# Which operand stands still: the gate and up products of a mixture of experts, f32, on one core

## The chip, the core and the metric

The kernel runs on one core of one Trainium2 chip. Its time is the device time of one execution in microseconds; of several runs the median is given. The engines are TensorE (matmul, with its weight loads listed apart as PEld), VectorE (DVE), ScalarE (ACT), GpSimd (POOL) and SyncE (SP, which here only issues transfers).

## What is computed

One block of a perceiver: attention from 2 x 512 tokens of 512 features to 2 x 8192 context rows, a windowed self-attention, and a mixture of experts. The change lies in the last part, which the reference writes as

```python
scores = jax.nn.sigmoid(h @ gate_w.T)
topk_score, topk_ids = jax.lax.top_k(scores.T, cap)        # cap = 128
xin = h[topk_ids]                                          # 16 experts x 128 tokens x 512
up = jnp.einsum('ecd,efd->ecf', xin, up_w) + up_b[:, None, :]
g = jnp.einsum('ecd,efd->ecf', xin, gw) + gb[:, None, :]
eo = jax.nn.silu(g) * up                                   # 2048 features per token
eo = jnp.einsum('ecf,edf->ecd', eo, down_w) + down_b[:, None, :]
flat = (eo * topk_score[..., None]).reshape(-1, Dm)
out = jnp.zeros_like(h).at[topk_ids.reshape(-1)].add(flat)
```

plus a shared expert that every token passes. All of it is f32.

## The kernel before

The program is one stream of stages. The attention to the context fills the span up to some 2640 us, the windowed attention goes up to some 2860 us, the shared expert up to 3033 us, and the sixteen experts take the rest. The source order, as the scheduler of the framework has laid it out per engine, sets the order of the work; each engine then runs its own list in order and waits for the others by semaphores. The two orders differ in places: transposes can come some matmuls earlier than the source has them.

An expert has 128 tokens, which is one tile. `gather(e)` fetches their rows from HBM by an indirect transfer on POOL's queue. `tokens(xin)` turns them with four transposes on TensorE and one copy on ScalarE (`transposed`, lines 94 to 99), so that features lie on partitions: `xinT` is 128 x 4 x 128.

The 2048 features of an expert's gate and up are worked in four quarters of 512 (`fq`). For each, `expert_in` loads one 1 MB tile of gate weights and one of up weights (`load_tile`, on SP's queue, nine buffers in two pools). Each of the two products is five matmuls into one PSUM bank `pf` of 128 tokens x 512 features. The first adds the bias: the stationary operand `pick` selects the expert's row, the moving operand `bias3` holds the biases, split in three bf16 parts on 96 partitions so that their sum is the f32 value. The other four, one for each 128 of the 512 input features, have the tokens `xinT` as stationary operand and 512 columns of weights as moving operand. ScalarE makes `sg`, the silu of gate (line 924), and VectorE multiplies it by up into `eo` (line 926).

`eo` has tokens on partitions, and the down product needs features there. So the loop at the end turns each quarter with four transposes and a copy on ScalarE into `eoT`, one quarter behind the products. After the fourth quarter `expert_out` makes the down product: a bias matmul from `pick` and `bias3`, sixteen matmuls of 512 columns with `eoT` stationary and four more weight tiles moving, a scaling by the token's score, and an indirect transfer that adds to the output.

The biases are made ready much earlier, beside the windowed attention, at places that `at(k, ...)` gives: `bias_in` fills `raw` with zeros and loads the rows three times on POOL's queue, and `bias_part` splits off one bf16 part on VectorE (a cast, a copy, and but for the last a subtraction). Gate's and up's rows are 2048 wide, down's 512. In the same stretch TensorE runs the windowed attention's own products, among them `pl` (line 624) and `plv` (line 634), the latent projections of keys and values, which wait for ScalarE and VectorE.

Of the kernel before, what the change touches and what calls it, by code (L numbers as in the profile page):

```python
# [10 lines left out]
F32 = mybir.dt.float32  # L11
I32 = mybir.dt.int32
U32 = mybir.dt.uint32
BF16 = mybir.dt.bfloat16
AF = mybir.ActivationFunctionType
ALU = mybir.AluOpType
# [3 lines left out]
P = 128  # L20
B, S, D = 2, 512, 512
# [4 lines left out]
DC = D // P  # L26
# [6 lines left out]
E, F, SH, CAP = 16, 2048, 1024, 128  # L33
FQ = F // 512
# [9 lines left out]
def perceiver_kernel(  # L44
# [8 lines left out]
    nc = tc.nc  # L53
# [40 lines left out]
    def transposed(dst, src, ps):  # L94

        tp = ps.tile([P, 4, P], F32, tag="ps", name="tp")
        for c in range(4):
            nc.tensor.transpose(tp[:, c, :], src[:, ts(c, P)], ident)  # L98
        nc.scalar.copy(dst, tp)
# [17 lines left out]
    with ExitStack() as es:  # L117
        cp = es.enter_context(tc.tile_pool(name="a_const", bufs=1))
        tmp = es.enter_context(tc.tile_pool(name="a_tmp", bufs=2))
# [8 lines left out]
        ps = first_ps.enter_context(tc.tile_pool(name="a_ps1", bufs=1, space=PSUM))  # L128
# [317 lines left out]
        for slot in range(NS + LAG):  # L446
            if slot == LAG:
                first_ps.close()
                steady_ps = ExitStack()
                ps = ps_q = steady_ps.enter_context(tc.tile_pool(name="a_ps", bufs=8, space=PSUM))  # L450
            if slot == NS + LAG - NKC:
                steady_ps.close()
                ps = es.enter_context(tc.tile_pool(name="a_ps3", bufs=7, space=PSUM))
# [51 lines left out]
    def load_tile(src):  # L505
        pool, tag = ((ctxp, "ctx"), (wpool, "w"))[loads[0] % 9 >= 4]
        loads[0] += 1
        t = pool.tile([P, 4, 512], F32, tag=tag, name="wt")
        nc.sync.dma_start(out=t, in_=src)
        return t  # L510

    ccp = ctx.enter_context(tc.tile_pool(name="c_const", bufs=1))
    ctmp = ctx.enter_context(tc.tile_pool(name="c_tmp", bufs=2))
    ps = ctx.enter_context(tc.tile_pool(name="c_ps", bufs=8, space=PSUM))
    dram = ctx.enter_context(tc.tile_pool(name="c_dram", bufs=1, space=bass.MemoryType.DRAM))
    h_dram = dram.tile([T, D], F32, name="h_dram")

    KB3 = 96  # L520
    FB = 2 * F + D
    pick = ccp.tile([KB3, E, P], BF16, name="pick")
    bias3 = ccp.tile([KB3, FB], BF16, name="bias3")
    gate_sb = ccp.tile([P, DC, E], F32, name="gate_sb")
    nc.gpsimd.dma_start(out=gate_sb, in_=gate.rearrange("(c p) e -> p c e", p=P))
    idx = ccp.tile([P, E], U32, name="idx")
# [12 lines left out]
    with ExitStack() as es:  # L539
        cp = es.enter_context(tc.tile_pool(name="b_const", bufs=1))  # L540
        tmp = es.enter_context(tc.tile_pool(name="b_tmp", bufs=2))
        gp = es.enter_context(tc.tile_pool(name="b_g", bufs=3))
        bp = es.enter_context(tc.tile_pool(name="b_bias", bufs=1))
# [12 lines left out]
        for h in range(4):  # L556
            r = slice(h * DK, (h + 1) * DK)
# [8 lines left out]
            out=band, in_=band, pattern=[[1, NK]], base=0, channel_multiplier=-1,  # L566
# [3 lines left out]
            out=band, in_=band, pattern=[[-1, NK]], base=W7 - 1, channel_multiplier=1,  # L570
# [160 lines left out]
        def at(k, f, *args):  # L731
            beside.setdefault(k, []).append(lambda: f(*args))
# [7 lines left out]
                pick[r], ident[r, ds(32 * i, E)].unsqueeze(2).to_broadcast([32, E, P])  # L740
            )

        def bias_in(src, n):
            raw = bp.tile([KB3, F], F32, name="raw")
            nc.gpsimd.memset(raw, 0.0)
            for i in range(3):
                nc.gpsimd.dma_start(out=raw[ds(32 * i, E), 0:n], in_=src)
            raws.append(raw)

        def bias_part(i, lo, n):  # L750
            raw = raws[-1]
            part = bp.tile([KB3, F], BF16, name="part")
            nc.vector.tensor_copy(part[:, 0:n], raw[:, 0:n])
            r = ds(32 * i, 32)
            nc.vector.tensor_copy(bias3[r, ds(lo, n)], part[r, 0:n])
            if i < 2:
                nc.vector.tensor_tensor(raw[:, 0:n], raw[:, 0:n], part[:, 0:n], ALU.subtract)

        def forward_in(n, key):

# [8 lines left out]
        lns, raws = {"b0": ln_b0}, []  # L769
# [2 lines left out]
            at(k, lambda n: attention_in(n, lns["b1"]), NT // B + i)  # L772
        for i in range(3):
            at(3 + 2 * i, picks, i)
        k = 9
        for src, lo, n in ((gb, 0, F), (up_b, F, F), (down_b, 2 * F, D)):
            at(k, bias_in, src, n)
            for i in range(3):
                k += 2
                at(k, bias_part, i, lo, n)  # L780
        at(29, norm, 0, "f0")
        for i, k in enumerate((31, 33, 35, 37)):
            at(k, forward_in, i, "f0")
# [5 lines left out]
        for k in range(len(items) + 3):  # L789
            i, n = divmod(k, NBQ)  # L790
# [54 lines left out]
    def gather(e):  # L845

        xin = ep.tile([P, D], F32, name="xin")
        nc.gpsimd.indirect_dma_start(  # L848
            out=xin, out_offset=None, in_=h_dram,
            in_offset=bass.IndirectOffsetOnAxis(ap=idx[:, e : e + 1], axis=0),  # L850
        )
        return xin

    def tokens(xin):
        xinT = ep.tile([P, DC, CAP], F32, name="xinT")
        transposed(xinT, xin, ps)
        return xinT
# [3 lines left out]
    tmp = ctmp  # L861
    ep = ctx.enter_context(tc.tile_pool(name="e_tmp", bufs=2))
    shd = [load_tile(sh_d[i]) for i in range(2)]
    norm(1, "f1")
    for b in range(B):
        sT = sTp.tile([P, SH // P, S], F32, tag="sT", name="sT")
        for f in range(SH // P):
            pair = []
            for wts in (shg, shu):
                pf = ps.tile([P, S], F32, tag="ps", name="pf")  # L870
                for c in range(DC):
                    nc.tensor.matmul(  # L872
                        pf, lhsT=wts[f // 4][:, c, ts(f % 4, P)], rhs=hT[b][:, c, :],
                        start=(c == 0), stop=(c == DC - 1),
                    )
                pair.append(pf)
            sg = st.tile([P, S], F32, name="sg")
# [7 lines left out]
            elif b == 1 and f == SH // P - 1:  # L885

                turned_lists()
                xin = gather(0)
# [3 lines left out]
        for j in range(4):  # L892
            po = ps.tile([P, D], F32, tag="ps", name="pso")
            for f in range(SH // P):
                nc.tensor.matmul(  # L895
                    po, lhsT=sT[:, f, ts(j, P)], rhs=shd[f // 4][:, f % 4, :],
                    start=(f == 0), stop=(f == SH // P - 1),
                )
            n = b * 4 + j
# [5 lines left out]
            elif j == 2:  # L905
                xinT = tokens(xin)

    def expert_in(e, fq, xinT):

        pair = []  # L910
        for src, lo in ((gw, 0), (up, F)):
            wt = ahead.pop(0) if ahead else load_tile(src[e, fq])
            pf = ps.tile([P, 512], F32, tag="ps", name="pf")
            nc.tensor.matmul(
                pf, lhsT=pick[:, e, :], rhs=bias3[:, ds(lo + fq * 512, 512)],
                start=True, stop=False,
            )
            for c in range(DC):
                nc.tensor.matmul(  # L919
                    pf, lhsT=xinT[:, c, :], rhs=wt[:, c, :], start=False, stop=(c == DC - 1)  # L920
                )
            pair.append(pf)
        sg = tmp.tile([P, 512], F32, name="sg")
        nc.scalar.activation(sg, pair[0], AF.Silu)  # L924
        eo = tmp.tile([P, 512], F32, name="eo")
        nc.vector.tensor_tensor(eo, pair[1], sg, ALU.mult)  # L926
        return eo

    def expert_out(e, eoT):
        py = ps.tile([P, D], F32, tag="ps", name="py")  # L930
        nc.tensor.matmul(
            py, lhsT=pick[:, e, :], rhs=bias3[:, ds(2 * F, D)], start=True, stop=False
        )
        for fq in range(FQ):
            wt = load_tile(down[e, fq])
            for c in range(4):
                nc.tensor.matmul(  # L937
                    py, lhsT=eoT[:, fq * 4 + c, :], rhs=wt[:, c, :],
                    start=False, stop=(fq == FQ - 1 and c == 3),
                )  # L940
        y = tmp.tile([P, D], F32, name="y")
        nc.vector.tensor_scalar(y, py, scol[:, e : e + 1], None, ALU.mult)  # L942
        nc.gpsimd.indirect_dma_start(  # L943
            out=out, out_offset=bass.IndirectOffsetOnAxis(ap=idx[:, e : e + 1], axis=0),
            in_=y, in_offset=None, compute_op=ALU.add,
        )

    eoT, done = None, None  # L950
    for k in range(E * FQ + 1):
        e, fq = divmod(k, FQ)
        if e < E:
            if fq == 0 and e > 0:
                xinT = nxt
            if fq == 0 and e + 1 < E:
                xin = gather(e + 1)
            eo = expert_in(e, fq, xinT)
        if k > 0:
            pe, pfq = divmod(k - 1, FQ)  # L960
            if pfq == 0:
                eoT = ep.tile([P, F // P, CAP], F32, name="eoT")
            transposed(eoT[:, ts(pfq, 4), :], done, ps)
            if pfq == FQ - 1:
                expert_out(pe, eoT)
        done = eo
        if fq == FQ - 1 and e + 1 < E:
            nxt = tokens(xin)

# [48 lines left out]
```

## Time and profile before

| | |
|---|---|
| Median of 3 runs | 3776.33 us (3776.25 to 3777.41) |
| Profiled execution | 3775.76 us, span 3774.0 us |
| Mean granted clock of TensorE | 0.996 |
| TensorE, matmuls busy | 3720.3 us, 99% of the span |
| VectorE / ScalarE / GpSimd busy | 2250.9 / 1614.9 / 2076.8 us |
| First gate matmul of the experts to the last down matmul | 3033.4 to 3764.6 us |
| Moved by DMA while the experts run | some 287 GB/s at a DMA share of 0.85 |

In a row of groups, the first number after the bar is the time in which at least one instruction of the group ran, the second the mean length of one in ns, and what follows the second bar is the idle time of the engine just before them and what ended it. A shape such as `128*128 128x512` gives the stationary operand (rows * columns) and the moving one. In the timeline the first number is the start, the second the length of a merged row, and `x5` the number of instructions in it. Of a matmul the end is modelled, so lengths overlap; the starts are measured. Busy time of TensorE is therefore no measure of how fast it works.

### The profile page before, as it was taken

How to read it: one execution, taken by the hardware profiler on the slowest of the kernel's cores; microseconds unless marked ns; L12 is line 12 of the kernel's file. 1: busy time of each engine (PE TensorE's matmuls, PEld its weight loads, DVE VectorE, ACT ScalarE, POOL GpSimd, SP SyncE). 2: the span in 40 equal slices, each digit the busy share in tenths (PEclk: the TensorE clock that was granted, in tenths of full speed). 3: DMA queues.
4: the chain of work that ended last, by engine and by line, in shares of the span. 5: the costliest groups of instructions: out<-in, count | busy, mean ns of one | idle time of the engine just before them, and what ended most of it. 6: DMA issues, size and time to landing. Idle time of an engine off the chain costs nothing.

```text
span 3774.0 us, 102663 instructions
## 1 busy us (share of the span) xinstructions
PE 3720.3 (99%) x44684; PEld 1854.2 (49%) x44684; DVE 2250.9 (60%) x5349; ACT 1614.9 (43%) x3020; POOL 2076.8 (55%) x562
## 2 busy tenths in 40 slices
PE   8999999999999999999999999999999999999998
PEld 4555555555555555555555555444454444444444
DVE  6877777777777777777777777687753500000000
ACT  2135555555555555555555555577462011111110
POOL 0059989998998998999899899500100000000000
PEclk9999999999999999999999999999999999999999
DMA  5322222122223432122222222122210178888885
GB/s 193 115 66 69 72 72 72 60 69 72 72 70 115 127 119 92 61 69 72 72 72 62 67 72 72 58 86 71 75 46 23 64 262 282 289 289 286 287 284 172
DMA packets 143748, 438.29 MB, mean 116 GB/s; under 512 B 9408, under 2 KB 11728, under 8 KB 117856
## 3 DMA queue, kind: packets, MB, share of 16 engines
q1 hardware_dynamic: 137856, 419.33, 33.5%
q0 software_dynamic: 5200, 12.30, 1.3%
q8 instruction: 350, 5.73, 0.6%
q14 instruction: 102, 0.84, 0.1%
q10 hardware_dynamic: 240, 0.08, 0.0%
HBM read 423.21 MB, written 8.47 MB: 114 GB/s over the span
## 4 chain that ended last, share of the span: by engine, by line
PE 94%; DVE 2%; ACT 2%; issue 1%; POOL 1%; DMA 0%; POOLq 0%; SPq 0%; ACTq 0%; DVEq 0%
PE sx L307 12%; PE pk L248 12%; PE sc L365 12%; PE pv L265 12%; PE av L389 11%; PE pf L919 11%; PE py L937 5%; PE pf L872 3%; PE sc L371 3%; PE sx L288 2%; PE avl L389 2%; PE pqkv L597 2%; PE pso L895 1%; PE po L106 1%; PE tp L98 1%
## 5 line engine op out<-in xcount | busy, mean ns | idle before, releaser
L403 POOL TENSOR_TENSOR acc<-acc,pt 128x2048 f32<-128x2048 f32 x437 | 1991.0, 4556 | 189.3 <-ACT pt L378 187.0
L378 ACT ACTIVATE pt<-sc,mbias 128x512 f32<-128x512 f32 x2016 | 1220.1, 688 | 943.4 <-PE sc L371 943.2
L312 DVE CUSTOM_DVE_ANT_0 junk<-sx,mk 128x512 bf16<-128x512 f32 x1776 | 1227.3, 691 | 538.6 <-PE sx L307 343.5
L365 PE MATMUL sc<-qT,kt 32*128 32x512 f32 x4096 | 548.3, 596 | 5.9 <-DVE vt L272 5.9
L265 PEld LDWEIGHTS pv<-wv_sb,ctx_t 128*32 128x32 f32 x16384 | 457.8, 110 | 178.9 <-DVE mst L312 106.2
L307 PE MATMUL sx<-kt,qT 32*128 32x512 f32 x3552 | 508.2, 640 | 0.9 <-DVE vt L272 0.9
L248 PE MATMUL pk<-ctx_t,wk_sb 128*32 128x256 f32 (+1 forms) x9216 | 499.7, 357 | 5.4 <-DMA ctx_t<-in_ctxT 3.1
L265 PE MATMUL pv<-wv_sb,ctx_t 128*32 128x128 f32 x16384 | 500.9, 273 | 2.1 <-DVE mst L312 2.1
L389 PE MATMUL av<-pt,vt 128*32 128x512 f32 x3528 | 471.2, 606 | 0.9
L919 PE MATMUL pf<-wt,xinT 128*128 128x512 f32 x1024 | 459.4, 593 | 1.1
L248 PEld LDWEIGHTS pk<-ctx_t,wk_sb 128*32 128x32 f32 x9216 | 284.3, 110 | 298.2 <-DVE mst L312 103.7
L365 PEld LDWEIGHTS sc<-qT,kt 32*128 32x128 f32 x4096 | 244.8, 184 | 190.5 <-issue 148.8
L926 DVE TENSOR_TENSOR eo<-pf,sg 128x512 f32<-128x512 f32 x64 | 44.3, 692 | 459.4 <-PE pf L919 450.9
L399 DVE TENSOR_TENSOR avs<-av,avs 128x512 f32<-128x512 f32 x441 | 302.5, 686 | 6.6 <-PE av L389 6.6
L919 PEld LDWEIGHTS pf<-wt,xinT 128*128 128x128 f32 x1024 | 193.0, 190 | 221.0 <-issue 213.2
L848 POOL DMA_INDIRECT xin<-h_dram,idx x16 | 15.9, 993 | 435.2 <-PE tp L98 310.0
L943 POOL DMA_INDIRECT out_x<-y,idx x16 | 25.2, 1575 | 408.8 <-DVE y L942 408.8
L252 ACT ACTIVATE kt<-pk,bk_c 128x256 f32<-128x256 f32 (+1 forms) x288 | 129.5, 450 | 224.1 <-PE pk L248 224.0
L937 PE MATMUL py<-wt,eoT 128*128 128x512 f32 x512 | 222.3, 592 | 0.0
L924 ACT ACTIVATE sg<-pf 128x512 f32<-128x512 f32 x64 | 38.2, 597 | 427.0 <-PE pf L919 427.0
L371 PE MATMUL sc<-mT,neg 32*128 32x512 bf16 x2048 | 209.5, 375 | 0.0
L389 PEld LDWEIGHTS av<-pt,vt 128*32 128x32 f32 x3528 | 69.5, 108 | 283.5 <-DVE mst L312 277.6
(167 smaller groups left out, 2559.6 us busy)
## 6 DMA issues: line engine op xcount, KB each, us to landing
ctx_t<-in_ctxT SPq DMA_DIRECT2D x160, 1024.0 KB, 6.2
wt<-in_gw SPq DMA_DIRECT2D x64, 1024.0 KB, 4.8
wt<-in_up SPq DMA_DIRECT2D x64, 1024.0 KB, 4.8
wt<-in_down SPq DMA_DIRECT2D x64, 1024.0 KB, 6.6
mk<-mrow SPq DMA_DIRECT2D x111, 256.0 KB, 3.6
ctx<-in_wqkv SPq DMA_DIRECT2D x3, 1024.0 KB, 5.1
mk<-mrow_h SPq DMA_DIRECT2D x17, 128.0 KB, 4.8
x_sb<-in_x SPq DMA_DIRECT2D x2, 1024.0 KB, 11.2
```

The source lines that it names most:

```text
L248: nc.tensor.matmul(pk[ts(h, DK), :], lhsT=wk_sb[:, c, ds(g * P + h * DK, DK)], rhs=ctx_t[slot, b][:, c, hs], start=(c == 0), stop=(c == DC ...
L265: nc.tensor.matmul(pv[ts(k, DK), i, :], lhsT=ctx_t[slot, b][:, c, ds((lo + i) * P + k * DK, DK)], rhs=wv_sb[:, c, ts(g, P)], start=(c == 0 ...
L307: nc.tensor.matmul(sm, lhsT=qT[r, g, ds(b * S + c * P, P)], rhs=k_t[s][r, :], start=True, stop=True)
L312: nc.vector.tensor_tensor_reduce(out=junk, in0=ss[h], in1=mk_t[s], scale=1.0, scalar=-3.0e38, op0=ALU.add, op1=ALU.max, accum_out=mst[u][: ...
L365: nc.tensor.matmul(sc, lhsT=k_t[s][r, ts(ch, P)], rhs=qT[r, g, ts(b, S)], start=True, stop=False)
L371: nc.tensor.matmul(ss[h], lhsT=neg[r, :], rhs=m_t[u][r, :], start=False, stop=True)
L378: nc.scalar.activation(pt[:, h, :], ss[h], AF.Exp, bias=mbias[:, b, cc : cc + 1], scale=SCALE)
L389: nc.tensor.matmul(av[ts(h, DK), :], lhsT=v_t[s][:, ch, ts(h, DK)], rhs=pt_t[s, ch][:, h, :], start=first or not last, stop=not last or (j ...
L399: nc.vector.tensor_tensor(avs[u], av, avs[u], ALU.add)
L403: eng.tensor_tensor(acc[u], acc[u], pt_t[s, ch], ALU.add)
L919: nc.tensor.matmul(pf, lhsT=xinT[:, c, :], rhs=wt[:, c, :], start=False, stop=(c == DC - 1))
L937: nc.tensor.matmul(py, lhsT=eoT[:, fq * 4 + c, :], rhs=wt[:, c, :], start=False, stop=(fq == FQ - 1 and c == 3),)
```

## The change

Gate and up change the operand that stands still. The weights' 128 x 128 blocks become stationary, and the 128 columns of `xinT` move, so that the result has features on partitions and tokens along the row. For each tile of weights there are now four blocks of features `j` with four matmuls each, 128 wide. The bias is then one value per partition: ScalarE adds gate's bias in its silu, and VectorE adds up's bias and multiplies in one instruction, each four times per quarter on 128 x 128. They write straight into `eoT`; the transposes and copies of `eo` fall away, and with them the lag of one quarter in the loop. Gate's and up's biases are loaded as 256 rows of 128 each and turned once with four transposes into `bias_c`; `bias3` keeps down's alone. The down product stays as it is.

```diff
-    FB = 2 * F + D
+    bias_c = ccp.tile([P, 4, P], F32, name="bias_c")
-    bias3 = ccp.tile([KB3, FB], BF16, name="bias3")
+    bias3 = ccp.tile([KB3, D], BF16, name="bias3")
...
-        def bias_in(src, n):
-            raw = bp.tile([KB3, F], F32, name="raw")
+        def bias_in():
+            rows = bp.tile([P, 4, P], F32, name="rows")
+            for i, src in enumerate((gb, up_b)):
+                nc.gpsimd.dma_start(
+                    out=rows[:, ts(i, 2), :],
+                    in_=src.rearrange("e (c p) -> (e c) p", p=P).rearrange("(n r) p -> r n p", r=P),
+                )
+            raw = bp.tile([KB3, D], F32, name="raw")
             nc.gpsimd.memset(raw, 0.0)
             for i in range(3):
-                nc.gpsimd.dma_start(out=raw[ds(32 * i, E), 0:n], in_=src)
-            raws.append(raw)
+                nc.gpsimd.dma_start(out=raw[ds(32 * i, E), :], in_=down_b)
+            raws.extend((rows, raw))
+
+        def bias_cols():
+            transposed(bias_c, raws[0].rearrange("r n p -> r (n p)"), ps)
...
-        k = 9
-        for src, lo, n in ((gb, 0, F), (up_b, F, F), (down_b, 2 * F, D)):
-            at(k, bias_in, src, n)
-            for i in range(3):
-                k += 2
-                at(k, bias_part, i, lo, n)
+        at(9, bias_in)
+        at(13, bias_cols)
+        for i in range(3):
+            at(15 + 2 * i, bias_part, i)
...
-    def expert_in(e, fq, xinT):
+    def expert_in(e, fq, xinT, eoT):
...
-            pf = ps.tile([P, 512], F32, tag="ps", name="pf")
-            nc.tensor.matmul(
-                pf, lhsT=pick[:, e, :], rhs=bias3[:, ds(lo + fq * 512, 512)],
-                start=True, stop=False,
-            )
-            for c in range(DC):
-                nc.tensor.matmul(
-                    pf, lhsT=xinT[:, c, :], rhs=wt[:, c, :], start=False, stop=(c == DC - 1)
-                )
+            pf = ps.tile([P, 4, CAP], F32, tag="ps", name="pf")
+            for j in range(4):
+                for c in range(DC):
+                    nc.tensor.matmul(
+                        pf[:, j, :], lhsT=wt[:, c, ts(j, P)], rhs=xinT[:, c, :],
+                        start=(c == 0), stop=(c == DC - 1),
+                    )
             pair.append(pf)
-        sg = tmp.tile([P, 512], F32, name="sg")
-        nc.scalar.activation(sg, pair[0], AF.Silu)
-        eo = tmp.tile([P, 512], F32, name="eo")
-        nc.vector.tensor_tensor(eo, pair[1], sg, ALU.mult)
-        return eo
+        sg = tmp.tile([P, 4, CAP], F32, name="sg")
+        for j in range(4):
+            i, k = divmod(e * (F // P) + fq * 4 + j, P)
+            nc.scalar.activation(
+                sg[:, j, :], pair[0][:, j, :], AF.Silu, bias=bias_c[:, i, k : k + 1]
+            )
+            nc.vector.scalar_tensor_tensor(
+                eoT[:, fq * 4 + j, :], pair[1][:, j, :], bias_c[:, 2 + i, k : k + 1],
+                sg[:, j, :], ALU.add, ALU.mult,
+            )
...
-            if pfq == 0:
-                eoT = ep.tile([P, F // P, CAP], F32, name="eoT")
-            transposed(eoT[:, ts(pfq, 4), :], done, ps)
-            if pfq == FQ - 1:
-                expert_out(pe, eoT)
-        done = eo
+            expert_in(e, fq, xinT, eoT[e])
+        if fq == 0 and e > 0:
+            expert_out(e - 1, eoT[e - 1])
         if fq == FQ - 1 and e + 1 < E:
             nxt = tokens(xin)
```

More of the change, by code (lines that the diff above doesn't have):

```diff
@@ L741, in picks, with bias_part @@
             )
-        def bias_in(src, n):
-            raw = bp.tile([KB3, F], F32, name="raw")
+        def bias_in():
[6 more added lines that the diff above has]
+            raw = bp.tile([KB3, D], F32, name="raw")
             nc.gpsimd.memset(raw, 0.0)
             for i in range(3):
-                nc.gpsimd.dma_start(out=raw[ds(32 * i, E), 0:n], in_=src)
-            raws.append(raw)
[L750 to L753, printed above, removed]
+                nc.gpsimd.dma_start(out=raw[ds(32 * i, E), :], in_=down_b)
+            raws.extend((rows, raw))
+        def bias_cols():
+            transposed(bias_c, raws[0].rearrange("r n p -> r (n p)"), ps)
+        def bias_part(i):
+            raw = raws[1]
+            part = bp.tile([KB3, D], BF16, name="part")
+            nc.vector.tensor_copy(part, raw)
             r = ds(32 * i, 32)
-            nc.vector.tensor_copy(bias3[r, ds(lo, n)], part[r, 0:n])
+            nc.vector.tensor_copy(bias3[r, :], part[r, :])
             if i < 2:
-                nc.vector.tensor_tensor(raw[:, 0:n], raw[:, 0:n], part[:, 0:n], ALU.subtract)
+                nc.vector.tensor_tensor(raw, raw, part, ALU.subtract)
         def forward_in(n, key):
@@ L906, in perceiver_kernel @@
                 xinT = tokens(xin)
-    def expert_in(e, fq, xinT):
+    def expert_in(e, fq, xinT, eoT):
         pair = []
-        for src, lo in ((gw, 0), (up, F)):
+        for src in (gw, up):
             wt = ahead.pop(0) if ahead else load_tile(src[e, fq])
-            pf = ps.tile([P, 512], F32, tag="ps", name="pf")
-            nc.tensor.matmul(
-                pf, lhsT=pick[:, e, :], rhs=bias3[:, ds(lo + fq * 512, 512)],
-                start=True, stop=False,
-            )
-            for c in range(DC):
-                nc.tensor.matmul(
-                    pf, lhsT=xinT[:, c, :], rhs=wt[:, c, :], start=False, stop=(c == DC - 1)
-                )
-            pair.append(pf)
-        sg = tmp.tile([P, 512], F32, name="sg")
-        nc.scalar.activation(sg, pair[0], AF.Silu)
-        eo = tmp.tile([P, 512], F32, name="eo")
-        nc.vector.tensor_tensor(eo, pair[1], sg, ALU.mult)
-        return eo
+            pf = ps.tile([P, 4, CAP], F32, tag="ps", name="pf")
[5 more added lines that the diff above has]
+                    )
+            pair.append(pf)
+        sg = tmp.tile([P, 4, CAP], F32, name="sg")
[3 more added lines that the diff above has]
+                sg[:, j, :], pair[0][:, j, :], AF.Silu, bias=bias_c[:, i, k : k + 1]
+            )
+            nc.vector.scalar_tensor_tensor(
+                eoT[:, fq * 4 + j, :], pair[1][:, j, :], bias_c[:, 2 + i, k : k + 1],
+                sg[:, j, :], ALU.add, ALU.mult,
+            )
     def expert_out(e, eoT):
@@ L931, in expert_out @@
         nc.tensor.matmul(
-            py, lhsT=pick[:, e, :], rhs=bias3[:, ds(2 * F, D)], start=True, stop=False
+            py, lhsT=pick[:, e, :], rhs=bias3, start=True, stop=False
         )
@@ L946, in expert_out @@
         )
-    eoT, done = None, None
+    eoT = {}
     for k in range(E * FQ + 1):
@@ L953, in perceiver_kernel @@
         if e < E:
[L954 to L960, printed above, removed]
-            if pfq == 0:
-                eoT = ep.tile([P, F // P, CAP], F32, name="eoT")
-            transposed(eoT[:, ts(pfq, 4), :], done, ps)
-            if pfq == FQ - 1:
-                expert_out(pe, eoT)
-        done = eo
+            if fq == 0:
+                eoT[e] = ep.tile([P, F // P, CAP], F32, name="eoT")
+                if e > 0:
+                    xinT = nxt
+                if e + 1 < E:
+                    xin = gather(e + 1)
+            expert_in(e, fq, xinT, eoT[e])
+        if fq == 0 and e > 0:
+            expert_out(e - 1, eoT[e - 1])
         if fq == FQ - 1 and e + 1 < E:
```

## The prediction

> **What bounds the kernel now.** I read the busy table first, then the slices, then the groups of the expert stage alone (from 3000 us to the end), then single stretches of it in the timeline.
>
> ```profile
> PE 3720.3 (99%) x44684; PEld 1854.2 (49%) x44684; DVE 2250.9 (60%) x5349; ACT 1614.9 (43%) x3020; POOL 2076.8 (55%) x562
> DMA  5322222122223432122222222122210178888885
> ```
>
> TensorE is busy for 99% of the span. In the last eight slices, the experts, the DMA row is at 8 while DVE, ACT and POOL (not shown) are at 0 or 1. The groups of that stage:
>
> ```profile
> L919 PE MATMUL pf<-wt,xinT 128*128 128x512 f32 x1024 | 459.4, 593 | 1.1
> L937 PE MATMUL py<-wt,eoT 128*128 128x512 f32 x512 | 222.3, 592 | 0.0
> L919 PEld LDWEIGHTS pf<-wt,xinT 128*128 128x128 f32 x1024 | 193.0, 190 | 221.0 <-issue 213.2 <-ACT xinT L99 4.7
> L914 PE MATMUL pf<-bias,pick 96*128 96x512 bf16 x128 | 46.3, 381 | 0.0
> L98 PE MATMUL tp<-ident,eo 128*128 128x128 f32 x256 | 40.9, 273 | 0.4 <-DVE eo L926 0.4
> L98 PE MATMUL tp<-ident,xin 128*128 128x128 f32 x64 | 9.6, 273 | 0.0
> ```
>
> Two things to see. The code issues 512 gate and up matmuls and 256 for down; the profile has 1024 and 512: an f32 matmul is two instructions, each with its own weight load. A transpose and a bf16 matmul are one. And the mean of 593 ns is no cost, since matmuls overlap; the cost is the distance between starts, which the timeline gives:
>
> ```profile
> 3417.66 0.38 PE L914 MATMUL pf<-bias,pick 96*128 96x512 bf16 x1
> 3417.89 2.31 PE L919 MATMUL pf<-wt,xinT 128*128 128x512 f32 x5
> 3418.32 0.19 PEld L919 LDWEIGHTS pf<-wt,xinT 128*128 128x128 f32 x1 [0.24 <-issue]
> 3418.75 0.19 PEld L919 LDWEIGHTS pf<-wt,xinT 128*128 128x128 f32 x1 [0.24 <-issue]
> ```
>
> A 512-wide f32 matmul starts every 0.429 us (five in 2.31 = 4 x 0.429 + 0.59), the bf16 bias matmul takes 0.22, and each load of 0.19 lies inside the matmul before it. Four transposes show as 0.60 us = 0.273 + 3 x 0.109, so 109 ns each.
>
> An expert's period, from those steps: 64 x 0.429 (gate, up) + 8 x 0.22 (their biases) + 16 x 0.109 (result turned) + 4 x 0.109 (tokens turned) + 32 x 0.429 + 0.22 (down) = 45.36 us. The starts of successive experts lie 45.70 apart; the other 0.34 is a wait for the turned tokens, under "A wait that grows".
>
> **What the Trainium skill says.** (1) "TensorE: Matmul & The Clock Gate", section "LDWEIGHTS (loading the stationary operand)": a load takes its columns / 1.2 ns, 107 for 128. The trace agrees once a fixed part is set aside: f32 loads last 110 ns for 32 columns, 174 for 109, 190 for 128, so 80 ns for 96 columns, or 0.83 each. Two loads issued together with no matmul between them start 108 ns apart at 128 columns and 92 at 109. (2) Same page, "The mechanism": a load overlaps a running matmul only if the row groups differ. Here it does not hold: the loads above use all rows and lie inside a running matmul of all rows. (3) Same page, "Back-to-back issue gap": a stream of load and matmul pairs, 128 wide, is given 81 ns a pair against 56 for the matmul alone: 25 ns of load left bare. This prices the slow rival. (4) "DMA: Bandwidth & Descriptors", "Where 436 GB/s comes from": a port ceiling of 435 GB/s. Short stretches of the trace reach 426.
>
> **The narrow matmul, which decides everything.** After the change gate and up take 4 x as many instructions, 4096, each 128 wide with its own 128-column load. The old stage has no f32 weight load of full speed beside so short a matmul. The nearest row is the latent projection of values in the windowed attention: 109-column loads, 128 wide, ten instructions in a row:
>
> ```profile
> 2716.09 1.16 PEld L634 LDWEIGHTS plv<-wlat_bd,ext 128*109 128x109 f32 x10
> 2716.20 1.25 PE L634 MATMUL plv<-wlat_bd,ext 128*109 128x128 f32 x10
> ```
>
> 1.25 = 0.272 + 9 x 0.109: the matmul sets the pace (a quarter of 0.429 is 0.107, and 2 ns more) and the 0.174 load costs nothing, loads overlapping each other too. With 128 columns the load rises to the same 108 as the matmul, so it is a close race. Lower bound: 0.1093, loads hidden. Upper bound: in the attention's turning of weights a 109-column load stands beside a 103-wide matmul (0.088 alone), and loads come every 0.096, which scaled by 128/109 is 0.1127. I take **0.111**.
>
> **Part by part.**
> - Removed per expert: 27.46 (wide matmuls) + 1.76 (biases) + 1.74 (turning the result). Added: 256 x 0.111 = 28.42. Net gain 2.54 us, x 16 = **40.7 us**. Ends: 256 x 0.1093 = 27.98 gives 47.8; 256 x 0.1127 = 28.85 gives 33.8.
> - **A wait that grows.** The compiled order of the new kernel puts the tokens' transposes directly before the next expert's gate matmuls. Today two bias matmuls and two transposes stand between:
>
> ```profile
> 3383.80 0.60 PE L98 MATMUL tp<-ident,xin 128*128 128x128 f32 x4
> 3384.24 0.60 PE L914 MATMUL pf<-bias,pick 96*128 96x512 bf16 x2
> 3384.48 0.59 ACT L99 COPY xinT<-tp 128x512 f32<-128x512 f32 x1
> 3385.12 0.30 PEld L919 LDWEIGHTS pf<-wt,xinT 128*128 128x128 f32 x2 [0.31 <-ACT xinT L99]
> ```
>
> The last token transpose starts at 3384.13, its copy ends at 3385.07, and the load follows. Of that, 0.66 us is covered and 0.34 is lost (0.23 until the load, 0.10 for the load itself). Afterwards nothing covers it: 3385.12 - 3384.13 is 0.99; less the transpose's own 0.109 and about 0.03 because ACT no longer copies a result just before, 0.85 lost. The load itself is then the weights', and is done early. Loss 0.51 x 15 boundaries = **-7.7 us** (bounds: 0.4 to 0.8 each, -6 to -12). Queued behind it on TensorE is all of gate and up; the loads on SP wait for those buffers, with nine tiles of slack.
> - The last expert: today TensorE waits 0.42 us (0.58 from start to start, less a transpose) for the last product before turning it. Afterwards down's first twelve matmuls, 10 us, cover the last products. **+0.6 us.**
> - ACT and DVE: per quarter of an expert four 128x128 silus and four products replace a 128x512 silu (597 ns), a copy (585) and a product (692). Nearest rows: 0.25 us for a 128x103 copy out of PSUM, 0.28 for a small DVE addition. Some 1.1 us on each engine beside 7.1 us of matmuls: free while under that; even doubled it is.
> - The biases' preparation, around 2650 to 2715: DVE loses six casts (1.21 us), six copies (1.2) and four subtractions (2.28) of 2048 columns, 24 us in all, where small ones remain. TensorE's waits from 2640 to 2720 us (total, times, longest):
>
> ```profile
> PE pl L624 <- ACT raw L607: 3.2, 3, 1.3
> PE plv L634 <- DVE ext L614: 2.6, 2, 1.6
> ```
>
> From 2720 on, without such work, the same waits are 0.55 and 0.30 each, so 5.8 - 3 x 0.55 - 2 x 0.30 = 3.5 us is excess; small pieces remain. I take **+3 us** (bounds 0 and 5.5, counting other waits there). Four transposes for the bias columns cost **-0.4**. On POOL two transfers in 512-byte pieces replace six wide ones (some 0.5 us of issue each) and two memsets of 1.8 us go; nobody on TensorE waits for POOL there.
>
> Sum: 40.7 - 7.7 + 0.6 + 3.0 - 0.4 = 36.2 us. The profiled execution took 3775.76 (span 3774.0 and 1.8 around it), 0.6 below the median of 3776.33. Against its own time the sum gives 3739.6, and set to the median **3740.1 us**.
>
> **The rivals.**
> - *The load is not hidden at 128 columns* (slower). Place: each of the 4096 pairs. Price: the skill's bare 25 ns on top of 0.109 makes 0.134: 4096 x 0.023 = 94 us more, **3834 us**. It decides from 36.2 / 4096 = 8.8 ns above my 0.111, that is 0.120 a pair. For it: the pair is at the edge, and long streams may show what ten do not. Against it: the ten above, 19 columns short of the case.
> - *The weights' transfers become the bound.* Today the stage moves 287 GB/s at a DMA share of 0.85; a period of 43.7 needs 287 x 45.7 / 43.7 = 300 at 0.89. Were 287 the ceiling, only the items outside the period would remain: 3776.3 - 3.2 = **3773 us**. Against it: stretches at 426 GB/s, and the queue that issues the loads waits for buffers (waits of SP's queue in the stage, total, times, longest):
>
> ```profile
> SPq L509 <- PE pf L919: 387.1, 108, 4.9
> SPq L509 <- PE py L937: 187.9, 60, 3.5
> ```
>
> - *The loads are hidden wholly* and the DVE relief is full: 3740 - 7 - 2.5 = 3730. This is the low end of my case.
>
> That the change doesn't do what it says is excluded by the compiled order: it has the 2048 narrow matmuls, and neither their bias matmuls nor the result's transposes.
>
> **How the numbers follow.** A measurement tells about 0.2% (7.6 us) from no change. My case, with the paces between 0.109 and 0.118: 0.86, all faster by more than that. Transfers as the bound, or a pace near 0.12: 0.05, no change. The bare load: 0.09, slower. Range: low 3729 (hidden loads, full relief). High: 0.1127 (+7), no relief (+3), boundary waits at 0.8 more (+4.5) give 3754; with a little for a pace beyond it, 3758.
>
> **What would show it.** In the new profile the narrow matmuls should start 0.109 to 0.113 apart, experts 43.7 apart, a wait of TensorE for the turned tokens of some 0.8 us should stand at 15 boundaries, and the first waits of the latent projections should fall to 0.3 and 0.55. A pace of 0.12 or more, or waits of TensorE for weights, would make the prediction wrong.

## The result and the profile after

The changed kernel takes 3744.03 us (median of 4 runs, 3743.6 to 3744.51) against 3776.29 of the kernel before beside it: a ratio of 0.9914 (95% interval 0.9902 to 0.9926), so 32.3 us less. The forecast was 3740.1 us, a gain of 36.2. The span of the profiled execution fell from 3774.0 to 3742.6 us, by 31.4.

The busy table and the groups of the expert stage (from 3000 us on) of the changed kernel:

```profile
PE 3682.9 (98%) x47376; PEld 2077.5 (56%) x47376; DVE 2256.2 (60%) x5525; ACT 1616.5 (43%) x3149; POOL 2071.3 (55%) x556
...
L924 PE MATMUL pf<-xinT,wt 128*128 128x128 f32 x4096 | 463.9, 275 | 10.1 <-ACT xinT L99 10.1
L924 PEld LDWEIGHTS pf<-xinT,wt 128*128 128x128 f32 x4096 | 461.0, 192 | 21.3 <-ACT xinT L99 13.7 <-issue 7.6
L948 PE MATMUL py<-wt,eoT 128*128 128x512 f32 x512 | 222.3, 592 | 0.0
L932 ACT ACTIVATE sg<-pf,bias_c 128x128 f32<-128x128 f32 x256 | 73.2, 368 | 566.1 <-PE pf L924 566.1
L935 DVE SCALAR_TENSOR_TENSOR eoT<-pf,bias_c,sg 128x128 f32<-128x128 f32 x256 | 72.1, 344 | 413.1 <-PE pf L924 413.1
```

The rows of gate's and up's bias matmuls and of the result's transposes are gone. The weight loads of gate and up, 193 us busy before, now fill 461, nearly as long as the matmuls. And a wait that was 4.7 us in the load row has become 13.7 there, 10.1 of which the matmul row shows too. The products on ACT and DVE take 73 and 72 us, or 1.14 and 1.13 per quarter, and TensorE never waits for them.

The list of TensorE's waits over the span names that wait (total, times, longest):

```profile
PE pf L924 <- ACT xinT L99: 10.1, 15, 0.7
```

The timeline at the start of a later expert shows the wait itself:

```profile
3367.91 0.60 PE L98 MATMUL tp<-ident,xin 128*128 128x128 f32 x4
3368.55 0.59 ACT L99 COPY xinT<-tp 128x512 f32<-128x512 f32 x1 [2.87 <-PE tp L98]
3369.19 1.53 PEld L924 LDWEIGHTS pf<-xinT,wt 128*128 128x128 f32 x13 [0.91 <-ACT xinT L99]
3369.19 1.60 PE L924 MATMUL pf<-xinT,wt 128*128 128x128 f32 x12 [0.68 <-ACT xinT L99]
```

The last transpose starts at 3368.24 and the first gate matmul at 3369.19, 0.95 later, with nothing between. Less the 0.109 that a transpose takes, 0.84 us are lost. (The list has 10.1 / 15 = 0.68, since it counts from the modelled end of the transpose.) Note the third row: the weight load has no need of the tokens, and yet it starts only when they are there, together with its matmul. So nothing covers this load; the next matmul starts after 0.213 us instead of 0.112, at all 15 boundaries. Why the load doesn't run ahead was not tried.

The pace in the stream comes from the last row: 1.60 = 0.275 + 11 steps, of which the first is 0.213, so 0.111 for the others. Over all consecutive starts of the stage the mean is 0.1117 us (0.11166 before rounding) once the 15 steps after a bare load are set aside, and the median 0.112. Experts follow each other every 43.91 us.

### The profile page after: what moved, and what is told of

Same layout as the page of the kernel before. It is cut to its first block, busy times and chain, and to the rows that moved or that the text cites. A ratio compares the mean times of both kernels' runs of the same rounds, so it can differ in the third digit from the quotient of the medians.

```text
span 3742.6 us, 108401 instructions
## 1 busy us (share of the span) xinstructions
PE 3682.9 (98%) x47376; PEld 2077.5 (56%) x47376; DVE 2256.2 (60%) x5525; ACT 1616.5 (43%) x3149; POOL 2071.3 (55%) x556
## 4 chain that ended last, share of the span: by engine, by line
PE 95%; ACT 1%; issue 1%; DVE 1%; DMA 1%; POOL 1%; POOLq 0%; SPq 0%; ACTq 0%
PE sx L307 12%; PE pk L248 12%; PE sc L365 12%; PE pv L265 12%; PE pf L924 12%; PE av L389 11%; PE py L948 6%; PE pf L880 3%; PE sc L371 3%; PE sx L288 2%; PE avl L389 2%; PE pqkv L598 2%; PE po L106 2%; PE pso L903 1%; PE pq L178 1%
## 5 line engine op out<-in xcount | busy, mean ns | idle before, releaser
L924 PE MATMUL pf<-xinT,wt 128*128 128x128 f32 x4096 | 463.9, 275 | 10.1 <-ACT xinT L99 10.1
L924 PEld LDWEIGHTS pf<-xinT,wt 128*128 128x128 f32 x4096 | 461.0, 192 | 21.3 <-ACT xinT L99 13.7
L935 DVE SCALAR_TENSOR_TENSOR eoT<-pf,bias_c,sg 128x128 f32<-128x128 f32 x256 | 72.1, 344 | 413.1 <-PE pf L924 413.1
L932 ACT ACTIVATE sg<-pf,bias_c 128x128 f32<-128x128 f32 x256 | 73.2, 368 | 566.1 <-PE pf L924 566.1
L307 PEld LDWEIGHTS sx<-kt,qT 32*128 32x128 f32 x3552 | 139.7, 182 | 138.1 <-issue 69.2
```

Source lines behind the costliest of these rows:

```text
L307: nc.tensor.matmul(sm, lhsT=qT[r, g, ds(b * S + c * P, P)], rhs=k_t[s][r, :], start=True, stop=True)
L924: nc.tensor.matmul(pf[:, j, :], lhsT=wt[:, c, ts(j, P)], rhs=xinT[:, c, :], start=(c == 0), stop=(c == DC - 1),)
```

## The experiments

**e1: the tokens turned earlier.** They are turned a quarter earlier, after the third pair of products.

```diff
-        if fq == FQ - 1 and e + 1 < E:
+        if fq == FQ - 2 and e + 1 < E:
             nxt = tokens(xin)
```

> The changed kernel with the next expert's tokens turned one quarter earlier, in the middle of the gate and up matmuls. Theory (a wait alone): the 0.84 us wait for the turned tokens and the 0.10 us of bare load after it vanish at 15 boundaries, 14.1 us, so 3744.0 - 14.1 = 3729.9 us, a period of 42.97 us. Rival (the weights' transfers are already near their bound): the period must move 12 tiles in 43 us, 305 GB/s in all; if they can't, TensorE waits for wt instead and the time stays within 3740 to 3744.

Measured: 3730.05 us, ratio to before 0.9877 (0.9862 to 0.9892). The wait is gone from the list of TensorE's waits, no other has come in its place in the expert stage, and experts follow each other every 42.97 us, as the theory had it. In the stretch from 3100 to 3700 us TensorE is busy throughout at a DMA share of 0.88 (columns: length, then busy time of PE, PEld, DVE, ACT, POOL, clock, DMA share, GB/s):

```profile
3100.00:3700.00 600.00, 600.00 (x4090) 492.23 (x4089) 73.58 (x238) 71.49 (x237) 32.99 (x25) 1.00 0.88 301
```

SP's queue still waited for buffers in the expert stage, 394.6 us on gate and up and 184.6 on down. So the 14.0 us between this version and the changed kernel were a wait and nothing else, the transfers are no bound at 301 GB/s, and this version beats both kernels.

**e2: fewer tokens moved.** The weight loads stay as they are; 112 or 64 of the 128 columns are moved and worked on. `eoT` takes turns in two buffers that are filled with zeros once, so the rest of it stays zero. The edit of the matmul for 112 columns (with 64 it has 64 in these places; ScalarE's and VectorE's instructions are narrowed in the same way):

```diff
-                        pf[:, j, :], lhsT=wt[:, c, ts(j, P)], rhs=xinT[:, c, :],
+                        pf[:, j, 0:112], lhsT=wt[:, c, ts(j, P)], rhs=xinT[:, c, 0:112],
...
```

> The changed kernel with 112 instead of 128 token columns moved in gate and up (16 of 128 tokens are left out there; the weight loads stay at 128 columns). Theory (the weight load sets the pace): matmuls still start 0.110 to 0.112 us apart, time 3736 to 3744 us. Rival (the matmul's own streaming sets the pace and the 0.112 is an overhead on it): 112 columns take 0.0958 to 0.098 us, 4096 x 0.014 to 0.016 = 57 to 66 us less, 3678 to 3687 us.

> The same with 64 token columns moved (half of the tokens left out in gate and up). Theory (load sets the pace): a floor of 0.108 to 0.112 us, time 3728 to 3744 us. Rival (matmul sets the pace): 0.056 us, 4096 x 0.056 = 229 us less, 3515 us. A load that can't start before the matmul ahead of it has begun and that must be whole before its own matmul would show 0.11 to 0.19.

Measured (one time each): 3744.36 us with 112, 3756.03 with 64. With 112, moving an eighth less took nothing off. The same three quarters of one expert, 192 gate and up matmuls in a row, in the changed kernel, with 112 and with 64 columns:

```profile
3214.73 21.60 PE L924 MATMUL pf<-xinT,wt 128*128 128x128 f32 x192
...
3214.95 21.59 PE L924 MATMUL pf<-xinT,wt 128*128 128x112 f32 x192
...
3220.85 21.55 PE L924 MATMUL pf<-xinT,wt 128*128 128x64 f32 x192
```

As 21.60 is 191 steps and one length of 0.275, a step is 0.1117 us. Over the whole stage, matmuls start 0.112 us apart at the median, whether 128, 112 or 64 columns move: the load sets the pace. The 12 us that 64 columns cost more are another matter. In two stretches the granted clock of TensorE was half (second and last row, against the first):

```profile
3050.00:3064.00 14.00, 13.32 (x120) 13.09 (x119) 1.72 (x8) 2.30 (x9) 0.95 (x1) 1.00 0.82 293
3065.00:3078.00 13.00, 13.00 (x46) 10.33 (x46) 0.86 (x4) 0.93 (x4) 0.00 (x0) 0.50 0.50 171
...
3335.00:3347.00 12.00, 12.00 (x42) 9.40 (x42) 0.86 (x4) 0.93 (x4) 0.00 (x0) 0.50 0.52 178
```

There are 46 matmuls in 13 us of such a stretch against 120 in the 14 us before it. By the clock record each stretch lasts 13.65 us, so half the pace loses some 13.7 us in all, near the 12 measured. Each begins 2.6 to 2.8 us after TensorE's wait for the tokens has ended at an expert's boundary:

```profile
3061.67 2.56 PE L924 MATMUL pf<-xinT,wt 128*128 128x64 f32 x21 [0.68 <-ACT xinT L99]
```

The other 13 boundaries have the same wait and no such stretch, and with 112 or 128 columns none of the 15 has one. So the wait alone does not bring it, the wait with 64 columns does at two of 15 boundaries, and what brought the clock down stays open. The time lies outside what both theories had; the distance between starts decides between them.

**e3: fewer weight columns loaded.** 96 of each 128 features are loaded and worked on; all 128 tokens move.

```diff
-                        pf[:, j, :], lhsT=wt[:, c, ts(j, P)], rhs=xinT[:, c, :],
+                        pf[0:96, j, :], lhsT=wt[:, c, ds(j * P, 96)], rhs=xinT[:, c, :],
...
```

> The changed kernel with 96 instead of 128 weight columns loaded for each gate and up matmul (a quarter of the features is left out there; all 128 token columns are moved). Theory (the load sets the pace at 128 columns): the load needs some 0.084 us now, the matmul's 0.1092 us takes over, 4096 x 0.0025 = 10 us less, 3734 us. Rival (a fixed overhead of each load and matmul pair): still 0.112 us, 3744 us.

Measured: 3733.45 us, ratio to before 0.9885 (0.9868 to 0.9901), 10.6 us less than the changed kernel. Starts lie 0.109 apart.

```profile
3212.29 21.12 PE L924 MATMUL pf<-xinT,wt 128*96 128x128 f32 x192
...
L924 PEld LDWEIGHTS pf<-xinT,wt 128*96 128x96 f32 x4096 | 449.2, 163 | 21.8 <-ACT xinT L99 13.7 <-issue 8.1
```

With the load shorter, the matmul's own 0.109 is the limit, so the 0.112 is no fixed overhead of each pair. e2 and e3 together: at 128 columns the load's pace is 0.0025 us slower than the matmul's, and only that shows.

**e4: the kernel before with its tokens turned earlier**, by the same edit.

> The kernel before with the tokens turned one quarter earlier, as in e1. Theory: its boundary loses 0.34 us (0.23 until the load, 0.10 of bare load), so 15 x 0.34 = 5.1 us less, 3771.2 us. Rival (the wait moves to another place, such as the copy of the turned result on ScalarE): no change, 3776 us.

Measured: 3771.91 us, ratio 0.9988 (0.9981 to 0.9994), 4.4 us less than the 3776.31 beside it. So in the kernel before, too, the wait was worth most of the 5.1 us that the theory gave it, and no other took its place. Experts follow each other every 45.36 us here. Where both kernels have their tokens early, the change is worth 41.9 us (3771.91 - 3730.05).

**e5: the kernel before without the bias matmuls of gate and up**, and with its tokens early, so that its boundary has no wait that the bias matmuls might cover.

```diff
-            nc.tensor.matmul(
-                pf, lhsT=pick[:, e, :], rhs=bias3[:, ds(lo + fq * 512, 512)],
-                start=True, stop=False,
-            )
...
```

> The kernel before with the tokens turned early (as e4) and without the 128 bias matmuls of gate and up (these two biases are left out). Theory: each costs its 0.22 us of TensorE, since nothing else bounds the stage: 28.2 us less than e4's 3771.9, 3743.7 us. Rival (the products' copies or the transfers take over in a shorter period): less than 20 us.

Measured: 3743.4 us, ratio to before 0.9911 (0.9895 to 0.9928), 28.5 us less than e4; experts follow each other every 43.61 us. So these matmuls cost 128 x 0.22 = 28.2 us in full, and they alone make two thirds of the 41.9. The transposes of the result are worth 256 x 0.109 = 27.9 us by their starts (no run takes them out alone), and the narrow matmuls cost 28.58 - 27.46 = 1.12 us more per expert, 18 in all. That makes 28.2 + 27.9 - 18 = 38 us, and the periods of e4 and e1 say the same: 16 x (45.36 - 42.97) = 38.2. The rest of the 41.9 lies outside these periods and in the spread of e4's runs (3770.4 to 3772.5).

**e6: the kernel before without the preparation of these biases**, their rows of `bias3` filled with zeros on GpSimd.

```diff
-        for src, lo, n in ((gb, 0, F), (up_b, F, F), (down_b, 2 * F, D)):
+        nc.gpsimd.memset(bias3, 0.0)
+        for src, lo, n in ((down_b, 2 * F, D),):
```

> The kernel before with the preparation of gate's and up's biases beside the windowed attention left out (their rows of bias3 are zero; their matmuls stay). Theory (part of TensorE's early waits was VectorE's bias work): the first expert matmul starts 1.9 us earlier than before, at 3031.5, with the waits at 2693 and 2702 us cut as in the changed kernel and the earlier ones as they are; time 3774.4 us. Rival (my prediction's step: all of the early excess is bias work): 3.5 us earlier, 3029.9, time 3772.8 us.

Measured: 3781.92 us, ratio 1.0014 (1.0007 to 1.0021): slower by 5.3 us, which neither theory had. The timeline shows why:

```profile
2661.33 0.55 DVE L90 TENSOR_SCALAR xn<-x_sb,mv,rs 128x512 f32<-128x512 f32 x1
2662.40 4.45 DVE L90 TENSOR_SCALAR xn<-x_sb,mv,rs 128x512 f32<-128x512 f32 x1
2662.62 3.95 POOL L776 MEMSET bias<- 96x4608 bf16 x1
2666.91 0.47 PE L98 MATMUL tp<-ident,xn 128*128 128x128 f32 x1 [4.31 <-DVE xn L90]
```

The fill that I put in stood beside a normalisation, which took 4.45 us instead of 0.55 and ended 0.3 us after the fill; TensorE waited 4.31 us for it. That is not all: while TensorE waited, its granted clock fell to half, from 2664.2 us on and for 10.24 us. A row from this stretch (columns as in e1):

```profile
2667.00:2674.00 7.00, 6.33 (x11) 2.81 (x12) 6.76 (x12) 0.85 (x2) 0.00 (x0) 0.50 1.02 422
```

Against the same matmuls of e7, which has neither the fill nor this stretch, TensorE falls behind by 4.0 us in the wait and by another 3.3 at half the clock; the two medians lie 7.5 apart. So e6 shows the price of the fill, and says nothing on the biases.

**e7: the same with nothing on GpSimd in its place**; the bias matmuls read down's biases.

```diff
-        for src, lo, n in ((gb, 0, F), (up_b, F, F), (down_b, 2 * F, D)):
+        for src, lo, n in ((down_b, 2 * F, D),):
...
-                pf, lhsT=pick[:, e, :], rhs=bias3[:, ds(lo + fq * 512, 512)],
+                pf, lhsT=pick[:, e, :], rhs=bias3[:, ds(2 * F, 512)],
```

> As e6, the kernel before without the preparation of gate's and up's biases, but nothing on GpSimd in its place: the 128 bias matmuls stay and read down's biases instead (gate's and up's biases are left out). In e6 a 3.95 us fill on GpSimd stood beside a normalisation on VectorE that took 4.45 instead of 0.55 us, and TensorE waited 4.3 us for it. Theory (a part of TensorE's early waits was bias work, the rest belongs to other VectorE and ScalarE work): the first expert matmul starts 1.5 to 2.2 us earlier than before, at 3031.2 to 3031.9, time 3774.4 us. Rival (my prediction's step: all the excess, 3.5 us, is bias work): 3029.9, 3772.8 us.

Measured: 3774.41 us, ratio 0.9995 (0.9986 to 1.0004), within the noise; the trace is sharper. The first expert matmul starts at 3032.0 us, 1.3 earlier than before. But 0.4 of this stands already at the end of the attention to the context, ahead of the waits in question. Counted from its last matmul, the first expert matmul comes after 403.0 us instead of 403.9: 0.9 earlier, under the 1.5 to 2.2 of the first theory and far under the 3.5 of the second. TensorE's waits from 2640 to 2720 us in this kernel, then in the changed kernel:

```profile
PE pl L624 <- ACT raw L607: 2.8, 3, 1.3
PE plv L634 <- DVE ext L614: 1.3, 2, 1.0
...
PE pl L625 <- ACT raw L608: 2.7, 3, 1.3
PE plv L635 <- DVE ext L615: 1.3, 2, 1.0
```

The kernel before has 3.2 and 2.6 there. So 1.7 to 1.8 us of these waits came from the preparation of gate's and up's biases, and the rest stays without it. One of those that stay can be read in the changed kernel: from 2681.9 us on TensorE waits 1.26 us for `raw`, which stood on ScalarE behind eight exponentials of the softmax.

## Why the prediction was right, and where its sizes were off

Direction, cause and range held; 3744.0 lies in 3729 to 3758. Three of the terms were too favourable and none too cautious, so no error hid another. By the prediction's steps:

- *The pace.* I took 0.111 us, and it is 0.1117. So 256 x 0.11166 = 28.58 us are added per expert, and against the 30.96 removed 2.38 remain: 16 x 2.38 = 38.1 us instead of 40.7. The step's argument was right: load and matmul are within 3 ns of each other, and of the two bounds the upper one, scaled from loads beside a 103-wide matmul, was nearer. e2 and e3 show it by both sides. The transposes, whose loads the prediction leaves out, would have misled: they too load 128 columns beside a 128-wide matmul and start every 0.109 us, but their loads last 0.141 us and not 0.19.
- *The wait that grows.* I had 0.51 us lost per boundary, and 7.7 in all. The wait was right (0.84 against 0.85), but "the load itself is then the weights', and is done early" was wrong: the load starts with its matmul, 0.10 us are bare again, and the loss is 0.84 + 0.10 - 0.34 = 0.60, or 9.0 us. e1 took back 14.0 / 15 = 0.93 per boundary.
- *The biases' preparation.* I took 3 us of relief less 0.4 for the transposes, and the runs show 0.9. The first expert matmul starts at 3031.9 us instead of 3033.4, but 0.6 of these 1.4 us stand already at the last matmul of the attention to the context (2628.86 instead of 2629.45), where the other profiled runs lie anywhere from 2628.6 to 2630.5. From there to the first expert matmul it is 403.1 us in the changed kernel and 403.9 before. Two things were wrong. My base of 0.55 and 0.30 per wait, taken from a later stretch, did not fit the early one, where other work delays ScalarE and VectorE: 1.8 us of waits went instead of 3.5, and the first waits fell to 0.90 and 0.65 on the mean, not to the 0.55 and 0.30 that I named as a sign. And half of the 1.8 was lost again. The last product of the windowed attention (`pow`) comes 1.8 us earlier in this count, but both kernels run a stretch of 13.65 us at half the granted clock here, which does not come earlier. From that last product to the stretch's end (before, then changed):

```profile
2843.20:2846.40 3.20, 3.20 (x12) 1.36 (x9) 0.00 (x0) 1.54 (x3) 0.00 (x0) 0.50 0.02 5
...
2840.80:2845.90 5.10, 5.10 (x14) 2.21 (x11) 0.00 (x0) 1.54 (x3) 0.00 (x0) 0.50 0.01 3
```

So the work behind it spends 1.9 us more at half the clock, which costs an estimated 1.0 us by these two rows; from the last product to the first expert matmul the changed kernel is 1.0 us slower (191.1 and 190.1). The 0.4 us for the transposes of the bias columns do not show: up to that last product the changed kernel takes as long as e7, which has none (212.0 us each).

- *The last expert*: TensorE's wait for the last product is gone from its list, +0.6 as worked out.

For the experts this makes 38.1 - 9.0 + 0.6 = 29.7 us; from the first expert matmul to the start of the last the traces have 730.6 and 700.8, which is 29.8. With 0.9 from the biases and the 0.6 from ahead of them it is 31.2, against 31.4 of the spans.

The slow rival, a bare load of 25 ns at each of the 4096 pairs, did not happen. The Trainium skill ("TensorE: Matmul & The Clock Gate", section "The mechanism") has a list in which a load overlaps only with matmuls of other row groups; here 4096 loads of all rows lie beside matmuls of all rows at a pace of 0.1117, and of 0.109 with 96 columns. The same section also names a background weight buffer whose loads run ahead; these loads would fit that, but no run here shows where they go.

The transfers as a bound are excluded by e1, at 301 GB/s. The section that the prediction names for its port ceiling of 435 GB/s ("DMA: Bandwidth & Descriptors", "Where 436 GB/s comes from") also says that for transfers from HBM a lower limit of some 358 binds. e1's mean stays under both. The stretches at 426 that the prediction names lie above the lower one, for 1.5 us each; no run here holds such a rate.

## What to carry to other kernels

When an operand is swapped so that a wide matmul becomes several narrow ones, compare the load of the stationary block with the streaming of the moving one by the distance between their starts, not by the length of a load in the profile: here a load of 190 ns that can start every 112 cost only 3 ns beside a matmul of 109. Count what the old form paid around the matmul, such as the bias and the turning of the result; it is their going that made the change pay here. And look at what stood between a producer and its consumer by chance: the removed matmuls had covered a copy, and moving the producer earlier was worth nearly half as much as the whole change (14.0 us against 32.3).

## What the runs showed of the hardware that was not expected

- An f32 weight load of 128 columns sets a pace of 0.112 us in a long stream whether the matmul beside it is 64, 112 or 128 columns wide, though two such loads alone start 0.108 apart. Where the 0.004 come from is open.
- With only half as many columns moved, two stretches of 13.65 us at half the granted clock appeared (e2, 64 columns), each soon after a wait of under 1 us, and with less work for the array the kernel was 12 us slower. Why they appeared was not tried.
- A wait of TensorE can cost more than its length: the 4.31 us of e6 came with 10.24 us at half the granted clock, which cost another 3.3 us. A gain can also be lost to such a stretch: half of the biases' relief went that way.
- A fill on GpSimd and an operation of VectorE that started 0.2 us before it excluded each other nearly wholly: the operation took 4.45 us instead of 0.55 (e6), and 0.53 in e7, where the fill is left out. The Trainium skill ("SBUF — State Buffer", section "Who interferes with whom") describes ports shared by the two engines as an exclusive lock that goes to whoever issues first; the exclusion fits, the order does not: by the stamps the operation that had started first was the one to wait. The kernel before has the same in small: a bf16 copy of 32x2048 there takes 2.37 us beside a fill of 1.80, and 0.68 elsewhere.
